# Three steps of the layer norm: from two GpSimd instructions to three ScalarE instructions, with new due times

## The chip, the core and the metric

The kernel runs on one core of a Trainium2 chip. Its five engines each have an in-order queue: TensorE (PE, with PEld for its weight loads), VectorE (DVE), ScalarE (ACT), GpSimd (POOL) and SyncE (SP), which here issues all DMAs. The metric is device time in microseconds of one execution; lower is better. The number shown is the median of several executions.

## What is computed

A decoder layer over 16 sequences of 256 positions and width 512. It has three parts, each added to its input and followed by a layer norm without gain or offset: a selective state-space scan (1024 channels, 16 states), a cross-attention over the feature axis (16 heads of 16 channels, sequences of 512), and a gated feed-forward part with quantized weights and activations. Cut to what matters:

```python
def _layernorm(x, axis=-1, eps=1e-05):
    m = jnp.mean(x, axis=axis, keepdims=True)
    v = jnp.var(x, axis=axis, keepdims=True)
    return (x - m) / jnp.sqrt(v + eps)

x = _layernorm(x + _L0_attn_ref(x, ...), axis=-1)    # state-space scan
x = _layernorm(x + _L0_xattn_ref(x, ctx_2048, ...), axis=-1)
x = _layernorm(x + _L0_ffn_ref(x, ...), axis=-1)
```

Inside the scan, per channel and state, `h[t] = exp(A*dt[t]) * h[t-1] + dt[t]*B[t]*u[t]`, and `y[t]` is the sum of `h[t]*C[t]` over the states.

## The kernel before, in words

A sequence (here: a batch) goes through four stages: `prep` (projections, a short convolution, the time steps), `scan`, `attn` (output projection, first norm, cross-attention, second norm) and `ffn` (feed-forward part, third norm). The stages of different batches overlap: while batch b is scanned, earlier batches are in attention and feed-forward.

The scan of a batch is cut into 32 units (8 channel tiles of 128 by 4 groups). A unit has 128 partitions of 32 channels by 4 states, and 4 states along the free axis. For a unit, a DMA brings `dtr` (time steps and products, broadcast from `dtd` in DRAM); POOL makes the first product `h <- bcr*dtr` (L657, recorded by the helper at L233); ACT makes the decays `dA` in PSUM (L668), two buffers; DVE runs two scans (L672); POOL makes the second product `h <- h*bcr` (L675, also L233). After four units PE sums over the states (L697), DVE gates (L705), and four of the seven `h` buffers are free again.

In attention PE makes scores (L830), DVE takes their maxima (L845), ACT makes exponentials (L889), PE forms the products with the values (L896). The casts L779, L781 and L854 split numbers into bf16 parts. The `rc` instruction L941 on POOL, once per batch, belongs to the softmax's denominators. The feed-forward weights are quantized once on the chip, in 24 pieces with two ACT instructions each (L439, L441). ACT changes its function table with an ACT_TABLE_LOAD, mostly around the softplus of `prep` (L595).

The order of each queue isn't written out by hand. The code makes tasks, each with a due time `t`, an engine, an estimated duration, the tasks that it comes after, and the buffers that it takes and frees. A planner, `run` (L167), goes through a clock of its own, and at each moment issues on every idle engine the ready task with the earliest due time, if its buffers are free and it isn't more than `AHEAD` beyond the earliest task not yet begun. A unit of due time is a scan unit, so a batch is 32 of them (`NSL`). The names in capitals at the top (L44 to L77) shift the due times: `KP`, `QP` and `VP` those of the attention's projections, `BCP` those of B and C in `prep`, `WEIGHP` that of the second product, `NORM`, `FFN` and `LNF` those of the second norm, the feed-forward part and the third norm, `WQ0` and `WQ` start and step of the weight quantization, `WS0` and `WS` those of the pass over the weights that finds their scale. What comes out of the planner is the order in each queue; on the chip every instruction then waits for what it needs.

The norm itself is `layernorm` (L451), called three times a batch, 48 times in all. DVE takes the statistics of two tiles of 128 positions (L458, L459); they lie in `lmv`, which holds mean and variance for each. `small` on POOL makes of them, on 128x2 numbers, the scale `lrs` and the offset `lnb`, in four instructions: L463 adds eps to the variance and takes the maximum with eps, L464 raises to the power -0.5, L465 changes the sign of the mean, L466 multiplies. ACT then applies scale and offset to the two tiles (L469).

Of the kernel before, what the change touches and what calls it, by code (L numbers as in the profile page):

```python
# [10 lines left out]
F32 = mybir.dt.float32  # L11
# [3 lines left out]
AF = mybir.ActivationFunctionType  # L15
ALU = mybir.AluOpType
# [4 lines left out]
P = 128  # L21
# [12 lines left out]
LN_EPS = 1e-5  # L34
# [15 lines left out]
OUT1 = 34.11  # L50
PSTEP = 2.02
TSP = 15.44
BCP = 9.29
KP = 34.45
QP = 37.76
VP = -3.68
SUMP = 0.16
WEIGHP = 1.88
FSTEP = 0.74
FUP = -0.18  # L60
BACK = 0.59

SHIFT = [(0, 0, 0, 0, 0, 0)] * 16
FDN = 14.54
LNF = 7.28
ATT = 39.73
SLAG = 7.79
GSTEP = 3.93
SCAN = -0.29
NORM = 81.05  # L70
FFN = 98.49
WQ = 3.57
WQ0 = 21.99
WS = 0.66
WS0 = 14.23
AHEAD = 12.29
HOP = 0.2  # L77
RINGS = {
    "xT": 2, "win": 2, "wr": 1, "wout": 1, "u": 4, "tmp": 2, "z": 2, "s": 3, "ts": 1, "bc": 1, "bcr": 3, "dtr": 4, "h": 7,
# [7 lines left out]
def decoder_kernel(ctx, tc, x, xT, ctx_in, mask, winT, wdtT, wbcT, wdpT, woutT, dvec, wqkvT, bqk, bv, wguT, wdnT, out):  # L87
    nc = tc.nc
# [16 lines left out]
    def const(shape, dt, s):  # L105
        return cp.tile(shape, dt, tag=s, name=s)
# [37 lines left out]
    def task(t, eng, us, fn, after=(), take=(), free=(), kb=0):  # L144
        if any(h.tag == "ps" for h in free) and eng in ("DVE", "ACT"):
            t -= BACK
        k = Task()
        k.t, k.i, k.eng, k.us, k.fn, k.take, k.free, k.kb = t, len(tasks), eng, us, fn, take, free, kb
        k.then, k.begun = [], False
        k.left = len(after)  # L150
        for p in after:
            p.then.append(k)
        for h in take:
            h.first = k
        for h in free:
            h.users += 1
        tasks.append(k)
        return k
# [5 lines left out]
    def dma(t, fn, after=(), take=(), free=(), kb=8):  # L164
        return task(t, "SP", 0.5, fn, after, take, free, kb)

    def run():  # L167
# [14 lines left out]
        while left:  # L182
# [10 lines left out]
            while f0 < len(front) and front[f0].begun:  # L193
                f0 += 1
            limit = front[f0].t + AHEAD
            any_ = False
# [56 lines left out]
    for i in range(RINGS["dA"]):  # L253

        t = ps.tile([P, 2, L], F32, tag=f"dA{i}", name=f"dA{i}", bufs=1)
# [7 lines left out]
    def cut(t, a, b):  # L263
        return t.rearrange("p (a b) -> p a b", a=a, b=b)
# [12 lines left out]
    nc.vector.memset(mhalf, -0.5)  # L277
    nmag = const([P, 1], F32, "nmag")
    nc.vector.memset(nmag, -MAGIC)
    pmag = const([P, 1], F32, "pmag")  # L280
    nc.vector.memset(pmag, MAGIC)

# [10 lines left out]
    for g in range(NB4):  # L293
# [7 lines left out]
        for n in range(1, NB4):  # L301
            t = cut(free["tmp"][n % 2][:, : NDT * NS // NB4], NDT, NS // NB4)
# [97 lines left out]
    def setup_w():  # L400
# [6 lines left out]
        for j in range(24):  # L407
            t = WS0 + WS * j
            h = Hold("hq")
# [8 lines left out]
        pb, hn = Hold("ps"), Hold("o")  # L418
        t = WS0 + WS * 24

# [13 lines left out]
        for j in range(24):  # L434
            t = WQ0 + WQ * j
            h, q = Hold("hq"), Hold("fw")
# [14 lines left out]
    def layernorm(t, hx, after):  # L451

        hst, hmv, hrs, hnb = (Hold(k) for k in ("lst", "lmv", "lrs", "lnb"))
        r = lambda: cut(hx.t, 2, H)

        def stats(i):
            st, mv = cut(hst.t, 2, 6), cut(hmv.t, 2, 2)
            nc.vector.bn_stats(st[:, i, :], r()[:, i, :])  # L458
            nc.vector.bn_aggr(mv[:, i, :], st[:, i, :])  # L459

        def small():
            mv, rs, nb = cut(hmv.t, 2, 2), hrs.t, hnb.t
            nc.gpsimd.tensor_scalar(mv[:, :, 1], mv[:, :, 1], LN_EPS, LN_EPS, ALU.add, ALU.max)  # L463
            nc.gpsimd.tensor_tensor(rs, mv[:, :, 1], mhalf, ALU.pow)  # L464
            nc.gpsimd.tensor_scalar(mv[:, :, 0], mv[:, :, 0], -1.0, None, ALU.mult)  # L465
            nc.gpsimd.tensor_tensor(nb, mv[:, :, 0], rs, ALU.mult)  # L466

        def scale(i):
            nc.scalar.activation(r()[:, i, :], r()[:, i, :], AF.Identity, bias=hnb.t[:, i : i + 1], scale=hrs.t[:, i : i + 1])  # L469

        s0 = task(t, "DVE", 0.85, lambda: stats(0), tuple(after[0]), (hst, hmv), (hst,))
        s1 = task(t, "DVE", 0.85, lambda: stats(1), (s0,) + tuple(after[1]), (), (hst,))
        m = task(t, "POOL", 1.35, small, (s0, s1), (hrs, hnb), (hmv,))
        return [task(t, "ACT", 0.79, lambda i=i: scale(i), (m,), (), (hrs, hnb)) for i in range(2)]

    S = [{} for _ in range(NB)]
# [17 lines left out]
    def prep(b):  # L494
# [72 lines left out]
        t_ts = task(t, "ACT", 0.37, lambda: nc.scalar.copy(hts.t, pts.t[:, :L]), (m,), (), (pts,))  # L567
        m = task(T + PREP + BCP, "PE", 1.1, bc, U + (t_wbc,), (p2, hbc, hp2))
        m = task(T + PREP + BCP, "ACT", 0.37, lambda: nc.scalar.copy(hp2.t, p2.t[:, :L]), (m,), (), (p2,))
        m = task(T + PREP + BCP, "PE", 0.5, lambda: nc.tensor.matmul(p3.t[:32, :L], sel4, hp2.t, start=True, stop=True), (m,), (p3,), (hp2,))  # L570
        m = task(T + PREP + BCP, "ACT", 0.36, lambda: nc.scalar.copy(hbc.t, p3.t[:32, :L]), (m,), (), (p3,))
        m = dma(t + 0.5, bc_store, (m,), (), (hbc,), 32)
# [41 lines left out]
    def scan(b):  # L614
# [29 lines left out]
        for d in range(NDT):  # L644
            hs, ws = [], []
            for g in range(NB4):
# [36 lines left out]
                for h2 in range(2):  # L683
                    ha = Hold("dA")
                    a = task(t - 0.6 + 0.5 * h2, "ACT", 0.92, lambda h2=h2, ha=ha, f=decay: f(h2, ha), (f,), (ha,), (hd,))
                    rs.append(task(t + 0.5 * h2, "DVE", 1.14, lambda h2=h2, ha=ha, f=run_: f(h2, ha), (a, p1), (), (ha,)))
                ws.append(task(t + WEIGHP, "POOL", 2.34, weigh, tuple(rs) + (st["t_C"],), (), (st["C"],)))
            pb = Hold("ps")
# [22 lines left out]
    def attn(b):  # L711
# [13 lines left out]
        for hf in range(2):  # L725
# [3 lines left out]
            for lt in range(2):  # L729
# [12 lines left out]
                m = task(t, "PE", 3.45, mult, (t_w,) + tuple(st["t_y"][4 * hf : 4 * hf + 4]), (pb,), (hw, st["u"][hf]))  # L742
                adds[lt].append(task(t, "DVE", 0.61, add, (m, t_x1), (), (pb,)))
        t_n1 = layernorm(U + OUT1 + 1.3, hr, adds)


# [40 lines left out]
        for m in range(2):  # L787
            qkproj(m, 1, T + KP + 1.05 * m)
        for m in range(2):
# [3 lines left out]
        for s in range(4):  # L793
            t = T + att + SLAG + VP + 0.7 * s
            pb = Hold("ps")
# [131 lines left out]
        no = (n0, n1)  # L927
        t = T + NORM + SHIFT[b][4]
        SO = tuple(t_so)
# [14 lines left out]
        for i in range(2):  # L944
# [9 lines left out]

            t_n.append([task(t, "POOL", 2.54, norm, (l,), (), (no[i],))])
        st["t_n2"] = layernorm(t + 1, hr, t_n)


    def ffn(b):
        st = S[b]  # L960
        T = b * NSL + FFN + SHIFT[b][5]
        hr = st["x"]
# [71 lines left out]
        for t in range(2):  # L1034
# [59 lines left out]
            m = m[0]  # L1094
            t_d.append([task(Et + 1, "DVE", 0.74, add, (m,), (), (pb, ho))])
        t_e = layernorm(E + LNF, hr, t_d)
        dma(E + LNF + 0.5, lambda: nc.sync.dma_start(out=out[b].rearrange("(k p) h -> p k h", p=P), in_=x2()), tuple(t_e), (), (hr,), 512)

# [54 lines left out]
def _build(v):  # L1153
    import numpy as np
    import concourse.bacc as bacc

    nc = bacc.Bacc("TRN2", target_bir_lowering=False, num_devices=1)
    arrays, args = {}, []
    for name, a in _layout(v):
        a = np.ascontiguousarray(a)  # L1160
        arrays[f"in_{name}"] = a
        args.append(nc.dram_tensor(f"in_{name}", a.shape, mybir.dt.from_np(a.dtype), kind="ExternalInput").ap())
    args.append(nc.dram_tensor("out_0", v["x"].shape, F32, kind="ExternalOutput").ap())
    with tile.TileContext(nc, schedule_with_timeline_sim=True) as tc:
        decoder_kernel(tc, *args)
    return nc, arrays
# [10 lines left out]
```

## Time and profile before

| | |
|---|---|
| median of 3 runs | 3010.79 us (3008.86 to 3011.28) |
| the profiled execution | 3007.98 us, span 3005.8 us |
| mean granted TensorE clock | 0.965 |
| DVE scans (L672) | 1024 x 1208 ns |
| POOL products (L233, 128x1024) | 1012 x 2363 ns |
| ACT decays (L668) | 2048 x 475 ns |
| POOL, norm: L463, L464, L465, L466 | 48 each: 231, 708, 228, 195 ns |
| ACT, norm: L469 | 96 x 806 ns |
| DVE, norm: L458, L459 | 96 each: 676, 182 ns |

The profile is of one execution. "Busy" is the time from an instruction's start to its end; instructions of one engine can overlap a little, so the distance from start to start can be shorter than the duration (a 128x1024 product on POOL takes 2363 ns and the next one starts 2.31 us after it). A wait is the idle time of an engine before an instruction, with the instruction that ended it. The chain of waits follows the last instruction back to what released it, step by step.

### The profile page before, as it was taken

What the parts mean: (1) busy time and instruction counts of PE and PEld (TensorE: products, weight loads), DVE (VectorE), ACT (ScalarE), POOL (GpSimd) and SP (SyncE); (2) the same over time, 40 slices, a digit from 0 to 9 for tenths busy, and PEclk for the clock granted to TensorE, in tenths of its full rate; (3) what the DMA queues carried; (4) which work ended last, traced back from release to release, by engine and by line L of the source; (5) the groups of instructions that cost most, each with busy time, mean ns of one, the idle gap of its engine ahead of it and who ended that gap; (6) DMA issues with size and microseconds to landing.
All of it is one profiled execution on the core that took longest, in us unless ns stands there. A gap on an engine that the chain in (4) does not pass through costs nothing.

```text
span 3005.8 us, 51881 instructions
## 1 busy us (share of the span) xinstructions
PE 2650.5 (88%) x17514; PEld 1319.4 (44%) x17514; DVE 2674.1 (89%) x4043; ACT 2334.0 (78%) x4731; POOL 2596.5 (86%) x1435
## 2 busy tenths in 40 slices
PE   6567888999989999898999989899998999999995
PEld 4333443454545445444444544444353544434333
DVE  6969888999989999898999989899999989999873
ACT  4787978787787878778787877878788787888674
POOL 3899999999898999989899998989989899999311
PEclk9787999999999999999999999999999999999998
DMA  6695776566465665746665574656646566564432
GB/s 215 222 305 182 233 224 205 188 199 206 143 218 182 204 195 171 224 138 214 193 200 186 168 224 150 216 189 196 189 157 226 165 203 193 187 203 147 125 98 71
DMA packets 363250, 567.46 MB, mean 189 GB/s; under 512 B 47316, under 2 KB 200024, under 8 KB 358888
## 3 DMA queue, kind: packets, MB, share of 16 engines
q1 hardware_dynamic: 362984, 564.16, 58.2%
q8 instruction: 137, 2.24, 0.3%
q14 instruction: 129, 1.06, 0.1%
HBM read 449.61 MB, written 114.43 MB: 188 GB/s over the span
## 4 chain that ended last, share of the span: by engine, by line
POOL 28%; PE 27%; DVE 16%; ACT 13%; issue 10%; DMA 5%; SPq 1%; POOLq 0%; ACTq 0%; DVEq 0%
POOL h L233 23%; DVE h L672 7%; PE bank L491 6%; ACT pT L889 4%; PE bank L697 4%; DVE mx L845 4%; PE av L896 3%; PE bank L830 3%; ACT dA L668 3%; PE bank L1013 3%; PE bank L763 2%; PE bank L799 2%; DMA dtr<-dtd 2%; ACT xres L469 1%; POOL s L233 1%
## 5 line engine op out<-in xcount | busy, mean ns | idle before, releaser
L672 DVE TENSOR_TENSOR_SCAN h<-dA,h 128x512 f32<-128x512 f32 x1024 | 1223.3, 1208 | 83.0 <-POOL h L233 41.2
L233 POOL TENSOR_TENSOR h<-h,bcr 128x1024 f32<-128x1024 f32 x512 | 1207.9, 2363 | 95.7 <-DVE h L672 92.9
L233 POOL TENSOR_TENSOR h<-bcr,dtr 128x1024 f32<-128x1024 f32 x500 | 1177.7, 2363 | 69.9 <-PE bank L697 63.4
L668 ACT ACTIVATE dA<-dtr,A 128x255 f32<-128x255 f32 x2048 | 963.9, 475 | 297.1 <-DVE h L672 255.6
L830 PE MATMUL bank<-qk 108*128 108x512 bf16 x2003 | 616.3, 385 | 78.9 <-DVE mx L845 44.7
L845 DVE TENSOR_REDUCE mx<-bank 128x1 f32<-128x512 f32 x1004 | 655.1, 675 | 25.8 <-PE bank L830 25.6
L889 ACT ACTIVATE pT<-bank 128x512 f32<-128x512 f32 x999 | 566.6, 590 | 119.1 <-PE bank L830 113.9
L491 PE MATMUL bank<-xT,win 128*128 128x256 f32 x1984 | 454.5, 382 | 20.4 <-DVE u L520 7.8
L896 PE MATMUL av<-pT,vaug 128*32 128x256 f32 x4096 | 336.2, 397 | 106.6 <-ACT pT L889 104.5
L491 PEld LDWEIGHTS bank<-xT,win 128*128 128x128 f32 x1984 | 377.2, 192 | 83.8 <-DVE u L520 9.5
L830 PEld LDWEIGHTS <-qk 108*128 108x128 bf16 x2048 | 179.7, 98 | 392.2 <-issue 264.2
L697 PE MATMUL bank<-h,sel 128*32 128x256 f32 x4096 | 262.0, 399 | 49.0 <-POOL h L233 48.9
L1013 PE MATMUL bank<-fw,xqT 128*128 128x512 fp8e4 x976 | 248.5, 381 | 12.5 <-DVE hq L1023 4.0
L896 PEld LDWEIGHTS av<-pT,vaug 128*32 128x32 f32 x4096 | 88.8, 109 | 356.8 <-ACT pT L889 277.9
L736 PE MATMUL bank<-wout,u 128*128 128x512 f32 x512 | 231.0, 595 | 4.9 <-DVE u L705 4.4
L697 PEld LDWEIGHTS bank<-h,sel 128*32 128x32 f32 x4096 | 124.1, 114 | 180.9 <-POOL h L233 72.2
L517 DVE SCALAR_TENSOR_TENSOR tmp<-bank,cw,tmp 128x254 f32<-128x254 f32 (+2 forms) x384 | 165.1, 468 | 7.8 <-ACT tmp L510 7.7
L1013 PEld LDWEIGHTS <-xqT 128*128 128x128 bf16 x1024 | 96.3, 98 | 151.4 <-issue 57.6
L736 PEld LDWEIGHTS bank<-wout,u 128*128 128x128 f32 x512 | 96.0, 190 | 108.5 <-issue 94.4
L1086 PE MATMUL bank<-fw,s 128*128 128x512 fp8e4 x496 | 127.0, 380 | 1.8 <-ACT s L1077 1.1
L233 POOL TENSOR_TENSOR s<-s,u 128x512 f32<-128x512 f32 x64 | 80.7, 1272 | 39.9 <-ACT s L595 39.9
L705 DVE TENSOR_TENSOR u<-bank,z 128x256 f32<-128x256 f32 x128 | 52.8, 413 | 60.9 <-PE bank L697 60.8
(157 smaller groups left out, 2961.7 us busy)
## 6 DMA issues: line engine op xcount, KB each, us to landing
dtr<-dtd SPq DMA_DIRECT2D x512, 256.0 KB
win<-in_winT SPq DMA_DIRECT2D x124, 512.0 KB
qk<-sqk SPq DMA_DIRECT2D x128, 384.0 KB
dtd<-s SPq DMA_DIRECT2D x64, 512.0 KB
wout<-in_woutT SPq DMA_DIRECT2D x32, 1024.0 KB
fw<-gu_q SPq DMA_DIRECT2D x64, 512.0 KB
sqk<-qf SPq DMA_DIRECT2D x64, 384.0 KB
bcr<-bcd SPq DMA_DIRECT2D x32, 512.0 KB
```

The source lines that it names most:

```text
L233: return nc.gpsimd.tensor_tensor(out, a, b, ALU.mult)
L491: nc.tensor.matmul(ps_t[:, i * L : (i + 1) * L], ws[:, k, i * P : (i + 1) * P], xt[:, k, :], start=k == 0, stop=k == 3)
L517: nc.vector.scalar_tensor_tensor(zi, pb.t[:, i * L : (i + 1) * L - s], cw[:, d0 + i, j : j + 1], zi, ALU.mult, ALU.add)
L668: nc.scalar.activation(ha.t[:, i, 1:], hd.t[:, 1:L], AF.Exp, scale=A[:, d, g, j : j + 1])
L672: nc.vector.tensor_tensor_scan(seg, ha.t.rearrange("p n l -> p (n l)"), seg, 0.0, ALU.mult, ALU.add)
L697: m = nc.tensor.matmul(pb.t[DB * g : DB * g + DB, :L], sel, cut(hs[g].t, J, L)[:, j, :], start=False, stop=j == J - 1, tile_position=(0, D ...
L736: nc.tensor.matmul(pb.t, u[:, i, lt * P : (lt + 1) * P], wo()[:, i, :], start=i == 0, stop=i == 3)
L830: nc.tensor.matmul(pb.t, qk()[:, j, side, c * P : (c + 1) * P], qk()[:, j, 1 - side, :], start=True, stop=True)
L845: task(t, "DVE", 0.62, lambda pb=pb, c=c, j=j: nc.vector.tensor_reduce(mx()[:, j, c : c + 1], pb.t, AX.X, ALU.max), (m,), (), (pb,))
L889: V["x"] = nc.scalar.activation(hp.t[:, j * H : (j + 1) * H], pb.t, AF.Exp, scale=DSC)
L896: i = nc.tensor.matmul(hav.t[32 * k : 32 * k + 32, :], vaug_f[:, c, c0 : c0 + 32], hp.t[:, j * H + h * L : j * H + (h + 1) * L], start=c == 0,
L1013: nc.tensor.matmul(pb.t, xqT()[:, i, t * P : (t + 1) * P], wu()[:, k, i, :], start=i == 0, stop=i == 3)
```

## The change

In `layernorm` the two POOL instructions L463 and L465 go. In their place a new task `signs` on ACT, with an estimated duration of 0.65, does three activations on the same 128x2 numbers: the sign of the mean, a Relu of the variance, and the addition of eps, whose bias is a new constant `leps`. It comes after the statistics, and `small`, now two instructions with an estimate of 0.9, comes after it. Eleven numbers that set due times change with it, and `AHEAD`.

```diff
-BCP = 9.29
-KP = 34.45
+BCP = 9.42
+KP = 34.95
-VP = -3.68
+VP = -3.24
-WEIGHP = 1.88
+WEIGHP = 2.11
-LNF = 7.28
+LNF = 7.66
-NORM = 81.05
-FFN = 98.49
-WQ = 3.57
-WQ0 = 21.99
-WS = 0.66
-WS0 = 14.23
-AHEAD = 12.29
+NORM = 82.79
+FFN = 99.13
+WQ = 2.31
+WQ0 = 23.46
+WS = 0.64
+WS0 = 16.0
+AHEAD = 15.36
...
+    leps = const([P, 1], F32, "leps")
+    nc.vector.memset(leps, LN_EPS)
...
+        def signs():
+
+            mv = cut(hmv.t, 2, 2)
+            nc.scalar.activation(mv[:, :, 0], mv[:, :, 0], AF.Identity, scale=-1.0)
+            nc.scalar.activation(mv[:, :, 1], mv[:, :, 1], AF.Relu)
+            nc.scalar.activation(mv[:, :, 1], mv[:, :, 1], AF.Identity, bias=leps)
+
         def small():
             mv, rs, nb = cut(hmv.t, 2, 2), hrs.t, hnb.t
-            nc.gpsimd.tensor_scalar(mv[:, :, 1], mv[:, :, 1], LN_EPS, LN_EPS, ALU.add, ALU.max)
             nc.gpsimd.tensor_tensor(rs, mv[:, :, 1], mhalf, ALU.pow)
-            nc.gpsimd.tensor_scalar(mv[:, :, 0], mv[:, :, 0], -1.0, None, ALU.mult)
             nc.gpsimd.tensor_tensor(nb, mv[:, :, 0], rs, ALU.mult)
...
-        m = task(t, "POOL", 1.35, small, (s0, s1), (hrs, hnb), (hmv,))
+        m = task(t, "ACT", 0.65, signs, (s0, s1), (), (hmv,))
+        m = task(t, "POOL", 0.9, small, (m,), (hrs, hnb), (hmv,))
```

## The prediction

> **What bounds the kernel now.** I read the page's engine totals first, then equal stretches of the span, then the waits of the steady part, then GpSimd's timeline around one norm, then the groups of small instructions.
>
> ```profile
> PE 2650.5 (88%) x17514; PEld 1319.4 (44%) x17514; DVE 2674.1 (89%) x4043; ACT 2334.0 (78%) x4731; POOL 2596.5 (86%) x1435
> POOL 3899999999898999989899998989989899999311
> ```
>
> Three engines are within 3% of each other and none is full. POOL's tenths stand at 8 or 9 and fall off only at both ends.
>
> ```profile
> core 0: us, PE busy (x) PEld busy (x) DVE busy (x) ACT busy (x) POOL busy (x), PEclk, DMA share, GB/s
> 375.00:550.00 175.00, 152.71 (x1028) 72.05 (x1028) 152.92 (x219) 145.02 (x294) 168.35 (x90) 0.95 0.65 207
> 1425.00:1600.00 175.00, 161.30 (x1084) 81.23 (x1083) 162.91 (x246) 139.59 (x288) 162.39 (x89) 0.99 0.59 192
> 2825.00:3006.00 181.00, 144.51 (x888) 63.67 (x880) 109.32 (x204) 107.08 (x191) 19.64 (x40) 0.92 0.32 102
> ```
>
> Early (second row) POOL leads at 168 of 175 us. In the steady part PE, DVE and POOL are equal at 161 to 163. In the last 181 us POOL has almost nothing to do, so what it is relieved of there is worth nothing.
>
> ```profile
> POOL h L233 <- DVE h L672: 71.4, 30, 4.8
> POOL h L233 <- PE bank L697: 43.4, 18, 3.5
> DVE h L672 <- POOL h L233: 21.2, 31, 1.0
> DVE h L672 <- ACT dA L668: 11.0, 30, 0.7
> ACT dA L668 <- DVE h L672: 168.5, 207, 2.7
> ```
>
> These are the waits between 900 and 2650 us (total, times, longest). POOL idles 114.8 us there, 11.6 us in each period of 177.1 us (the rc instruction L941 starts at 1680.52, 1857.69, 2034.92 us). It waits for DVE's scans and for PE, which holds the h buffers. DVE waits for POOL as well: the engines take turns at being late.
>
> ```profile
> 1341.77 0.23 POOL L463 TENSOR_SCALAR lmv<-lmv 128x2 f32<-128x2 f32 x1
> 1342.08 0.71 POOL L464 TENSOR_TENSOR lrs<-lmv,mhalf 128x2 f32<-128x2 f32 x1
> 1342.85 0.23 POOL L465 TENSOR_SCALAR lmv<-lmv 128x2 f32<-128x2 f32 x1
> 1343.16 0.20 POOL L466 TENSOR_TENSOR lnb<-lmv,lrs 128x2 f32<-128x2 f32 x1
> 1343.31 2.36 POOL L233 TENSOR_TENSOR h<-h,bcr 128x1024 f32<-128x1024 f32 x1
> ```
>
> One norm holds POOL from 1341.77 to 1343.31, 1.54 us, with no wait inside.
>
> **What is removed.** L463 and L465 cost 0.31 us each from start to next start. That is 0.62 us a norm, three norms a period: 1.86 us of 177.1, and 48 x 0.62 = 29.8 us in all. Adding start-to-start durations along POOL's built order gives 2578.4 us up to the last h product before and 2552.4 after: 26.0 us can count, the rest lies in the tail, where POOL idles.
>
> **What is added.** Three activations on 128x2 a norm. No such row exists.
>
> ```profile
> L414 ACT ACTIVATION_READ_ACCUMULATOR hq<-hq 128x1 f32 x24 | 4.5, 186 | 0.0
> L854 ACT ACTIVATE ml<-bank 8x128 bf16<-8x128 f32 x242 | 61.6, 254 | 3.4 <-DVE bank L859 1.3 <-PE bank L874 0.9
> L595 ACT ACT_TABLE_LOAD x31 | 39.8, 1283 | 0.6
> L439 ACT ACTIVATE hq<-hq,pmag,wiv 128x1024 f32<-128x1024 f32 x24 | 29.5, 1234 | 7.2 <-DMA hq<-in_wdnT 3.7 <-DMA hq<-in_wguT 3.5
> ```
>
> The nearest in width is the 128x1 read at 186 ns, the next the 8x128 activation at 254 ns: 0.56 to 0.76 us a norm if each ends before the next starts. I take 0.56, since width sets more than rows; it is 27 us of ACT in all (upper end 36). ACT has 139.6 of 175 us busy, so its total covers this. If that cover fails, 1.7 us a period falls on ACT's followers.
>
> The Trainium skill's page "ScalarE: Activation LUTs" (Rules for kernel authors) speaks against the edit: relu, add and multiply belong on VectorE. By its section on what a table load costs (186 ns fixed, 93 ns more for a pointer operand, 93 ns overlap), my estimate is 0.47 to 0.66 us for the three; no run here shows that. The trace stands against it here: in the steady row above DVE is busy 162.9 of 175 us and ACT 139.6, so VectorE has 23 us less room.
>
> **The new wait.** The three stand in ACT's in-order queue and wait for the second statistics (L459). Behind them in the built order come decays (L668), exponentials (L889) and casts (L854, L779); DVE's scans wait for the first, PE's value products for the second. The hop itself is short: L459 ends at 2998.88 and L463 starts at 2998.97, 0.09 us. A norm's latency becomes 1.54 - 0.62 + 0.56 + 0.09 = 1.57 us, so the tail's norms and the last one change by nothing.
>
> **What moves.** The due times are changed too, so every queue has another order. The counts below come from the two built orders with the trace's start-to-start durations (h product 2.31 us, scan 1.13, score maximum 0.60).
>
> Head: ACT's work ahead of the first decay goes from 23.8 to 27.2 us, as there are two table loads more (65 against 63) and one tanh earlier; and SP's queue has the 0.77 MB of wqkv ahead of the first dtr, which was behind it. POOL's first product waits for that dtr now (4.87 us). I take +3.5; ends 0 (all hidden) and +8 (wqkv at the 171 GB/s of the first 45 us is 4.6 more).
>
> Batch 1: of the 48 quantizing activations (L439, L441, about 1.1 us each) 44 fall into it, against 23. ACT's queue there grows from 133.4 to 158.0 us and passes POOL's 153.9. Now batches 1 and 2 take 158.6 and 169.2 us, 4.1 and 7.7 more than their fullest queue (POOL 154.5 and 161.5). Batch 1 thus becomes 162 to 166: +3.5 to +7, I take +5. Batch 2 has POOL at 160.2: -1.
>
> Batches 3 to 14: POOL's queue falls from 164.3 to 162.4 a batch, DVE's stays 163.6, PE's 160.3. But the work comes in larger lumps. Before, the most DVE work from one scan unit to the next is 10.3 us; after, it is 13.3 (batches 4 to 7) and 13.9 (9 to 14), and GpSimd's order changes from one repeated pattern to two. To weigh this I cut a batch into stretches of eight scan units, take in each the longest of the ACT, DVE and POOL queues, and average over where the cuts lie. Before this gives 175.6 us a batch, against 177.1 measured, so it follows the trace within 1%. Summed over batches 3 to 14 the change is -0.7 us; with POOL level with the scans instead of one unit behind, +3.5; with stretches of four units, -4.1 and +23.7. I take +4; ends -4 and +24. The 1.86 us a period are thus given back: in a shorter POOL queue the wait for DVE and PE grows.
>
> Last batch and tail: after the last scan DVE has 122.8 us left before and 122.2 after, PE 160.9 and 160.3: 0.
>
> Sum: +3.5 + 5 - 1 + 4 + 0 = +11.5 us. On the profiled execution's 3007.98 us (span 3005.8 and 2.2 around it) this is 3019.5; that execution lies 2.8 us below the median of 3010.79, on which the sum gives 3022.3. I take 3020 us.
>
> **Rivals.** *The relief is kept.* If the lumps are absorbed by the seven h buffers, only DVE and POOL matter. The largest lead of a POOL product over its scan and back within a batch is 8.5 us before, and 8.0 (batches 4 to 7) and 9.5 (9 to 14) after. Batch by batch, POOL's queue plus this gives 16.7 us less over batches 1 to 14, or 26 if no wait grows: 2994, at best 2985. For it: POOL is 168 of 175 early, and ACT has room. Against it: in the steady part POOL already waits for two engines whose work stays.
>
> *Swallowed exactly.* Steady -4, head and batch 1 half hidden (+4): 3011. For it: the tables above cancel almost to zero. Against it: the ACT queue of batch 1 has no cover.
>
> *ACT's lumps reach the scans.* There are two dA buffers, so decay and scan cannot drift more than two scans apart. If the stretches of four units are right, +24, with 3.5 + 5 - 1 of head and first batches: 3010.8 + 31.5 = 3042. It decides if DVE waits for dA more than 3 us a period (now 11.0 us in ten). Against it: the wait is small now with lumps of 10 us.
>
> The edit itself not being made is excluded: the built order has 48 times three activations, and 96 GpSimd instructions fewer.
>
> **How the numbers follow.** 0.2% is 6 us, about what a measurement of this kernel can tell from no change. Forecast (given back, and the start paid: 3012 to 3032) 0.37; lumps reach the scans 0.17; swallowed 0.14; kept 0.32. A time over 3016.8 takes nearly all of the first two: slower 0.52. Faster, under 3004.8: 0.33. Within: 0.15. The forecast's own range is 3012 to 3032. Cases of both signs hold most of the chance, so the range reaches from 2986 (nearly all of the relief) to 3045 (all lumps, the head near its upper end).
>
> **What would show it.** Right: POOL idles over 13 us in a steady period and the period is 176 to 178 us; batch 1 takes over 162 us with ACT leading; the first h product starts after 52 us. Wrong: a steady period under 175.5 us means that the relief is kept; activations of the norm over 0.3 us each, or waits of the scans for dA over 3 us a period, mean the third rival; an unchanged start falsifies the head.

## The result, and the profile after

| | before | after |
|---|---|---|
| median | 3011.03 us (3008.86 to 3011.81, 4 runs) | 3040.3 us (3034.92 to 3042.04, 4 runs) |
| ratio | | 1.0096, 95% interval 1.0082 to 1.011 |
| span of the profiled execution | 3005.8 us | 3040.2 us |
| mean granted TensorE clock | 0.965 | 0.960 |

The changed kernel is 29 us slower, 1%. The lines below stand against those of the kernel before; the eight new lines of code make L668 into L676, L672 into L680, L697 into L705, and the norm is now L460 to L476. First the page: the engine totals, GpSimd's tenths (the busy share of each fortieth of the span), and the chain of waits by engine (before, that chain was POOL 28%, PE 27%, DVE 16%, ACT 13%, DMA 5%).

```profile
PE 2682.7 (88%) x17514; PEld 1323.3 (44%) x17514; DVE 2676.0 (88%) x4044; ACT 2356.5 (78%) x4877; POOL 2574.1 (85%) x1339
...
POOL 3899999999898999989898997989899798989211
...
DVE 31%; PE 23%; POOL 19%; DMA 10%; issue 9%; ACT 7%; SPq 1%; POOLq 0%; ACTq 0%; DVEq 0%
```

POOL has 96 instructions and 22.4 us of busy time less (48 times the 231 and 228 ns of the two steps), ACT 146 instructions and 22.5 us more (144 activations and two table loads): the move itself is there. Yet the span is 34 us longer, and GpSimd's steady part shows sevens where there were eights and nines. Next the equal stretches:

```profile
core 0: us, PE busy (x) PEld busy (x) DVE busy (x) ACT busy (x) POOL busy (x), PEclk, DMA share, GB/s
...
200.00:375.00 175.00, 143.21 (x861) 67.14 (x861) 148.17 (x203) 157.51 (x291) 168.50 (x78) 0.87 0.76 247
375.00:550.00 175.00, 156.21 (x1056) 74.06 (x1058) 158.93 (x232) 138.53 (x300) 173.22 (x89) 0.96 0.63 195
1425.00:1600.00 175.00, 158.17 (x1075) 79.20 (x1074) 162.34 (x244) 137.73 (x293) 159.79 (x83) 0.99 0.60 190
2825.00:3006.00 181.00, 157.36 (x998) 64.18 (x990) 119.89 (x219) 116.01 (x228) 27.72 (x39) 0.95 0.33 104
```

The same stretch of 200 to 375 us before, which the prediction does not show:

```profile
200.00:375.00 175.00, 147.75 (x876) 70.75 (x875) 154.92 (x218) 144.23 (x279) 166.65 (x81) 0.89 0.69 226
```

From 200 to 375 us ACT is busier, as predicted (157.5 us; before 144.2), but POOL is at 168.5 and leads. In the steady part (1425 to 1600 us) PE does 3.1 us less in 175 us than before, POOL 2.6 (of which 1.4 are the steps moved away, three norms of 0.46) and DVE 0.6: nobody has become the bound, and the engines wait more. The last row still holds work that was done by then before. The waits from 900 to 2650 us (total, times, longest) say for whom:

```profile
ACT dA L676 <- DVE h L680: 133.7, 160, 3.5
...
POOL h L233 <- DVE h L680: 88.7, 44, 4.7
...
POOL h L233 <- PE bank L705: 55.7, 34, 2.9
...
ACT hq L1024 <- PE bank L1021: 46.7, 44, 2.6
DVE mx L853 <- PE bank L838: 38.9, 36, 2.7
...
PE bank L705 <- POOL h L233: 34.1, 28, 2.9
...
DVE h L680 <- POOL h L233: 13.8, 18, 1.4
```

Three of the same waits before, which the prediction does not show:

```profile
PE bank L697 <- POOL h L233: 11.5, 10, 1.6
ACT hq L1016 <- PE bank L1013: 11.4, 20, 0.7
...
DVE mx L845 <- PE bank L830: 8.1, 29, 0.4
```

POOL waits 17 us more for the scans and 12 more for PE's sums. But PE's sums also wait for POOL (34.1; before 11.5), DVE's maxima for PE's scores (38.9; before 8.1), and ACT's `hq`, made of a result of the feed-forward part, for PE (46.7; before 11.4). Each of these engines is late for another one.

Where the 34.4 us of span went, read from the start of every 32nd second product on POOL (one batch each; the differences are taken before rounding):

| stage | before | after | difference | predicted |
|---|---|---|---|---|
| start to the first second product | 57.2 | 64.3 | +7.1 | +3.5 (0 to 8) |
| batch 0 | 140.0 | 137.8 | -2.1 | not counted |
| batch 1 | 158.6 | 160.3 | +1.7 | +5 (3.5 to 7) |
| batch 2 | 169.2 | 160.8 | -8.4 | -1 |
| batches 3 to 14 | 2119.9 | 2147.8 | +28.0 | +4 (-4 to 24) |
| batch 15, to the last second product | 155.3 | 162.0 | +6.7 | 0 |
| tail | 205.8 | 207.2 | +1.4 | 0 |

### The profile page after: what moved, and what is told of

Same layout as the page of the kernel before. It is cut to its first block, busy times and chain, and to the rows that moved or that the text cites. A ratio compares the mean times of both kernels' runs of the same rounds, so it can differ in the third digit from the quotient of the medians.

```text
span 3040.2 us, 51841 instructions
## 1 busy us (share of the span) xinstructions
PE 2682.7 (88%) x17514; PEld 1323.3 (44%) x17514; DVE 2676.0 (88%) x4044; ACT 2356.5 (78%) x4877; POOL 2574.1 (85%) x1339
## 4 chain that ended last, share of the span: by engine, by line
DVE 31%; PE 23%; POOL 19%; DMA 10%; issue 9%; ACT 7%; SPq 1%; POOLq 0%; ACTq 0%; DVEq 0%
POOL h L233 16%; DVE h L680 13%; DVE mx L853 8%; PE bank L705 5%; PE bank L499 4%; PE bank L838 3%; PE av L904 2%; ACT dA L676 2%; ACT pT L897 2%; DVE tmp L525 2%; PE bank L1021 2%; DMA qk<-sqk 2%; DVE hq L1033 1%; DVE hq L1031 1%; PE bank L744 1%
## 5 line engine op out<-in xcount | busy, mean ns | idle before, releaser
L680 DVE TENSOR_TENSOR_SCAN h<-dA,h 128x512 f32<-128x512 f32 x1024 | 1220.0, 1207 | 58.0 <-POOL h L233 28.7
L676 ACT ACTIVATE dA<-dtr,A 128x255 f32<-128x255 f32 x2048 | 966.5, 475 | 254.7 <-DVE h L680 206.4
L853 DVE TENSOR_REDUCE mx<-bank 128x1 f32<-128x512 f32 x999 | 648.5, 675 | 58.4 <-PE bank L838 57.5
L838 PE MATMUL bank<-qk 108*128 108x512 bf16 x1996 | 626.3, 388 | 79.3 <-DVE mx L853 35.2
L499 PE MATMUL bank<-xT,win 128*128 128x256 f32 x1984 | 464.3, 388 | 19.5 <-ACT hq L416 14.3
L499 PEld LDWEIGHTS bank<-xT,win 128*128 128x128 f32 x1984 | 382.5, 195 | 92.1 <-ACT hq L416 14.6
L904 PE MATMUL av<-pT,vaug 128*32 128x256 f32 x4096 | 334.3, 399 | 67.1 <-ACT pT L897 64.3
L705 PE MATMUL bank<-h,sel 128*32 128x256 f32 x4096 | 273.5, 412 | 61.1 <-POOL h L233 60.5
L705 PEld LDWEIGHTS bank<-h,sel 128*32 128x32 f32 x4096 | 127.3, 117 | 200.2 <-POOL h L233 91.3
L1024 ACT ACTIVATE hq<-bank,fhc 128x512 f32<-128x512 f32 x122 | 83.1, 684 | 65.8 <-PE bank L1021 64.9
L702 PE MATMUL bank<-u,diag 32*32 32x256 f32 x1024 | 85.4, 405 | 51.8 <-DVE z L646 24.3
```

Of the source, the lines that this page charges most:

```text
L499: nc.tensor.matmul(ps_t[:, i * L : (i + 1) * L], ws[:, k, i * P : (i + 1) * P], xt[:, k, :], start=k == 0, stop=k == 3)
L676: nc.scalar.activation(ha.t[:, i, 1:], hd.t[:, 1:L], AF.Exp, scale=A[:, d, g, j : j + 1])
L680: nc.vector.tensor_tensor_scan(seg, ha.t.rearrange("p n l -> p (n l)"), seg, 0.0, ALU.mult, ALU.add)
L705: m = nc.tensor.matmul(pb.t[DB * g : DB * g + DB, :L], sel, cut(hs[g].t, J, L)[:, j, :], start=False, stop=j == J - 1, tile_position=(0, D ...
L838: nc.tensor.matmul(pb.t, qk()[:, j, side, c * P : (c + 1) * P], qk()[:, j, 1 - side, :], start=True, stop=True)
L853: task(t, "DVE", 0.62, lambda pb=pb, c=c, j=j: nc.vector.tensor_reduce(mx()[:, j, c : c + 1], pb.t, AX.X, ALU.max), (m,), (), (pb,))
```

## The norm itself, after

ACT's timeline around one norm in the steady part, then POOL's:

```profile
1527.97 0.20 ACT L466 ACTIVATE lmv<-lmv 128x2 f32<-128x2 f32 x1 [0.51 <-DVE lmv L461]
1528.08 0.19 ACT L467 ACTIVATE lmv<-lmv 128x2 f32<-128x2 f32 x1
1528.30 0.29 ACT L468 ACTIVATE lmv<-lmv,leps 128x2 f32<-128x2 f32 x1
1528.50 0.55 ACT L518 ACTIVATE tmp<-bank,cw 128x256 f32<-128x256 f32 x1
```

```profile
1529.26 0.70 POOL L472 TENSOR_TENSOR lrs<-lmv,mhalf 128x2 f32<-128x2 f32 x1
1530.04 0.20 POOL L473 TENSOR_TENSOR lnb<-lmv,lrs 128x2 f32<-128x2 f32 x1
1530.19 2.39 POOL L233 TENSOR_TENSOR h<-h,bcr 128x1024 f32<-128x1024 f32 x1
```

The three activations last 0.20, 0.19 and 0.29 us, 0.68 in all, but the second starts before the first has ended and the next instruction before the third has: from the first start to the next instruction's start it is 0.53 us (predicted 0.56). POOL is held from 1529.26 to 1530.19, 0.93 us instead of 1.54, so 0.61 is saved (predicted 0.62). ACT waited 0.51 us for the statistics here; over the whole run that wait is 15.0 us in 20 times. In the last norm of all, the time from the end of the last statistics to ACT's `xres` is 1.75 us (3033.26 to 3035.01) against 1.72 before.

The estimate from the Trainium skill's page "ScalarE: Activation LUTs" (What ACT_TABLE_LOAD costs) was 0.47 to 0.66 us for the three. Its parts are near the rows: 186 ns fixed against 190 and 197 measured, and 93 more for an operand against the 296 ns of L468, which has the bias `leps`. The overlap of 93 ns shows between the first step and the second, but not between the second and the third, which starts 0.03 us after the second has ended.

So the move costs and saves what the rows of before said. The question is the 29 us.

## Experiments

The change does two things at once: it moves two steps, and it changes twelve planner numbers and the tasks, so that every queue gets another order. Theory 1: the order makes it slower, and the move alone is a gain. Theory 2: the three activations and their wait for the statistics hold up ScalarE's in-order queue, and so the rest.

**The order alone, first by its numbers.** The kernel before, with the twelve new numbers (`BCP` to `AHEAD`) and nothing else of the change.

```diff
-BCP = 9.29
+BCP = 9.42
...
-AHEAD = 12.29
+AHEAD = 15.36
```

> The twelve new numbers (eleven due times and AHEAD) with the norm as before, four steps on GpSimd. Theory 1 (the order that the due times make costs the time): 3030 to 3050 us, near the changed kernel's 3040. Theory 2 (the three activations and the new wait on ScalarE cost it): 3005 to 3016 us, like before.

3077.39 us, 1.0218 of before (1.0198 to 1.0238). The direction is theory 1's, the size more than expected: with four POOL steps the new numbers cost 66 us, more than the whole change. It is an order of its own, though: without a task on ACT for the norm, the planner doesn't arrive at the changed kernel's.

**The move with the old numbers.** The changed code (its own ACT task `signs`) with the twelve old numbers. The planner sees an ACT task more and makes a third order of it, again one repeated pattern.

```diff
-NORM = 82.79
+NORM = 81.05
...
-AHEAD = 15.36
+AHEAD = 12.29
```

> The three steps on ScalarE as their own task, with all twelve numbers as before; the planner makes an order of its own from them. Theory 1: 2995 to 3025 us, on either side of before, since a third order comes out and only its lumps decide. Theory 2: 3030 us or more.

3031.76 us, 1.0065 (1.0048 to 1.0081). Old numbers don't bring the old order back, and this order too is slower than before's. It lies 7 us above theory 1's range and within theory 2's, so this run alone does not part the two. The new numbers can't be all of the loss: both plans made with the ACT task lie above before.

**The move at exactly the old order.** The three activations are emitted inside the POOL task `small`, so the planner plans what it did before; the two GpSimd steps are gone. Apart from these steps every queue has before's order, instruction by instruction.

```diff
-            nc.gpsimd.tensor_scalar(mv[:, :, 1], mv[:, :, 1], LN_EPS, LN_EPS, ALU.add, ALU.max)
+            nc.scalar.activation(mv[:, :, 0], mv[:, :, 0], AF.Identity, scale=-1.0)
+            nc.scalar.activation(mv[:, :, 1], mv[:, :, 1], AF.Relu)
+            nc.scalar.activation(mv[:, :, 1], mv[:, :, 1], AF.Identity, bias=leps)
             nc.gpsimd.tensor_tensor(rs, mv[:, :, 1], mhalf, ALU.pow)
-            nc.gpsimd.tensor_scalar(mv[:, :, 0], mv[:, :, 0], -1.0, None, ALU.mult)
```

> Every queue in exactly the order of before; the two GpSimd steps of the norm are gone and the three activations stand in ScalarE's queue at that place. Theory 1: the move by itself is harmless and worth part of the 26 us of GpSimd: 2985 to 3011 us. Theory 2: 3025 us or more, with the scans waiting for dA more than now.

2994.31 us, 0.9939 (0.9918 to 0.9961): faster than both kernels, 16.6 us under the 3010.93 of before in the same session, and 46 under the changed kernel, which does the same instructions in another order. Its waits from 900 to 2650 us:

```profile
POOL h L233 <- DVE h L675: 80.2, 34, 4.8
POOL h L233 <- PE bank L700: 43.5, 16, 3.5
...
DVE mx L848 <- PE bank L833: 11.7, 23, 1.8
ACT hq L1019 <- PE bank L1016: 11.4, 20, 0.7
...
DVE h L675 <- ACT dA L671: 10.0, 23, 0.7
...
PE bank L700 <- POOL h L233: 6.9, 6, 1.4
```

POOL's wait for the scans has grown by 9 us in 1750 against before (it is done earlier), and the rest is as before. The longer waits that the changed kernel shows among PE, DVE, POOL and ACT are absent.

**Exactly the new order, without the move.** The changed kernel with `signs` empty and the four steps back on POOL; all else in its order.

```diff
         def signs():
-            mv = cut(hmv.t, 2, 2)
-            nc.scalar.activation(mv[:, :, 0], mv[:, :, 0], AF.Identity, scale=-1.0)
...
+            pass
...
+            nc.gpsimd.tensor_scalar(mv[:, :, 1], mv[:, :, 1], LN_EPS, LN_EPS, ALU.add, ALU.max)
             nc.gpsimd.tensor_tensor(rs, mv[:, :, 1], mhalf, ALU.pow)
+            nc.gpsimd.tensor_scalar(mv[:, :, 0], mv[:, :, 0], -1.0, None, ALU.mult)
```

> Every queue in exactly the order of the changed kernel, but with the norm's four steps on GpSimd and none on ScalarE. Theory 1: the order stays, and GpSimd is 26 us fuller: 3040 to 3065 us. Theory 2: 3011 to 3025 us, since ScalarE is free of the three steps.

3075.76 us, 1.0209 (1.0191 to 1.0227), 11 us above theory 1's range and far from theory 2's. With this the square is closed:

| | old order | new order | order costs |
|---|---|---|---|
| four steps on POOL | 3011 (before) | 3076 | +65 |
| two on POOL, three on ACT | 2994 | 3040 (after) | +46 |
| the move brings | -17 | -35 | |

The move is a gain in both orders, the order a loss with both sets of steps. In the new order the move brings 35 us, about twice as much as in the old one; that this is more than the 29.8 us of POOL that it takes away lies within the noise of the two ratios (some 7 us). One line of the waits of this kernel shows what it shortens there:

```profile
ACT xres L473 <- POOL lnb L470: 41.0, 28, 2.3
```

In the changed kernel the same wait is 10.0 us, and 20.0 in the run below without the three activations: in the new order ACT stands at the scaled tiles until POOL's four steps are through, and with two of them less it stands there half as long. How much of the 35 us this makes was not tried.

**ScalarE's steps alone, in both orders.** The two kernels with the move, each without its three activations: the sign of the mean and eps are left out of the computation.

```diff
-            nc.scalar.activation(mv[:, :, 0], mv[:, :, 0], AF.Identity, scale=-1.0)
-            nc.scalar.activation(mv[:, :, 1], mv[:, :, 1], AF.Relu)
-            nc.scalar.activation(mv[:, :, 1], mv[:, :, 1], AF.Identity, bias=leps)
```

> The order of before in every queue, the two GpSimd steps gone and the three activations of the norm gone too: sign and eps are left out of the computation. Theory order (the three activations cost next to nothing, the order costs all): 48 x 0.68 = 33 us of ScalarE go, on an engine that is busy 78% of the span, so the time stays within 6 us of the run with the three activations at this order (2994.3): 2988 to 2997. Theory wait (what stands behind the three activations on ScalarE is held up by their wait for the statistics): it falls by 10 us or more, under 2984.

> The changed kernel's order in every queue, with the three activations of the norm left out (sign and eps are not computed). Theory order: within 10 us of the changed kernel (3040.3): 3030 to 3042, and about as far above the run of the old order without activations as the changed kernel lies above the old order with them (46 us). Theory wait (in this order the three activations stand ahead of decays that the scans need, so the wait for the statistics is the loss): 20 us or more below the changed kernel, under 3020, and the gap between the orders shrinks to 25 us or less.

Old order: 2985.18 us, 0.9917 (0.9902 to 0.9932), 9 us under the kernel with the activations. That lies between the two expectations, and the intervals of the two ratios overlap, so it is a cost of some 9 us and not a sharp one. New order: 3038.95 us, 1.0098 (1.0081 to 1.0115), 1.4 us under the changed kernel, which is nothing that can be told. The gap between the orders is 54 us without the activations, not smaller than with them. Theory 2 falls for the changed kernel: no ScalarE step of the norm and no wait for the statistics makes its loss.

**What in the new order costs it.** Three suspicions, each tried as a pair: the same relief in the old order (with the move) and in the changed kernel. If the relieved resource is what the new order runs short of, the changed kernel gains far more than the other. Called B, C and D: TensorE, VectorE, and the stores of `qf` (projected queries and keys) to DRAM and back, which the chain of waits of the changed kernel passes in the steady part. In the expectations A stands for GpSimd and the scans as the pace of both orders, E for a loss among the compute engines alone.

```profile
2168.92 5.01 DMA sqk<-qf
2173.93 0.01 issue
2173.94 5.98 DMA qk<-sqk
2179.92 0.14 issue
2180.06 0.81 PE bank L838 x3
```

B leaves out a quarter of the input projections (three of four k slices; 512 matmuls L499 less):

```diff
-            for k in range(4):
+            for k in range(3):
```

> Order of before with the three activations (the 2994 us kernel), and every projection by 3 of its 4 slices of the inner dimension (a quarter of it is left out): TensorE has 512 passes of 0.22 us less, 113 us, 7 us a batch. Theory A (in either order GpSimd and the scans pace it): 2985 to 2996 us. Theory B (TensorE being late is what the new order pays): a little less here too, 2975 to 2990.

> The changed kernel with the same quarter of the projections left out. Theory A: 3025 to 3040 us, a gain like that of the old order, under 15 us. Theory B: 2970 to 3005 us, a gain of over 35 us and more than twice that of the old order, since the scores behind the state sums in TensorE's queue come earlier.

2979.85 us in the old order (0.99, 0.9884 to 0.9917), 14 less than with all four; 3049.27 in the new one (1.0139, 1.0118 to 1.016), 9 more. The old order's time lies within what B had for it, the new order's outside both ranges; a gain in the new order above that of the old, B's sign, is absent. The relief was smaller than meant, though: 76 us of busy time in the old order (2643.7 to 2568.0) and 62 in the new one (2682.7 to 2620.8), against 113. The stretch from 900 to 2650 us of the changed kernel, and of the changed kernel with the relief:

```profile
900.00:2650.00 1750.00, 1602.74 (x10645) 797.91 (x10646) 1610.89 (x2413) 1381.95 (x2903) 1582.70 (x820) 0.99 0.59 186
```

```profile
900.00:2650.00 1750.00, 1553.96 (x10273) 741.28 (x10272) 1597.94 (x2399) 1365.41 (x2879) 1569.23 (x814) 0.96 0.58 185
```

With less to do, TensorE was granted 0.96 instead of 0.99, and the other engines got through less as well. So this is weak evidence against B: the relief was partly given back.

C takes the score maxima over 384 of 512 columns:

```diff
-nc.vector.tensor_reduce(mx()[:, j, c : c + 1], pb.t, AX.X, ALU.max)
+nc.vector.tensor_reduce(mx()[:, j, c : c + 1], pb.t[:, :384], AX.X, ALU.max)
```

> Order of before with the three activations, and the score maxima over 384 of 512 columns (the rest is left out): VectorE has about 1024 x 0.13 = 136 us less, 8.5 us a batch. Theory C (VectorE's lumps pace the steady part): 2950 to 2975 us. Theory A with GpSimd alone: 2985 to 2994.

> The changed kernel with the maxima over 384 columns. Theory C (the larger lumps of VectorE are what the new order pays): 2960 to 2995 us, a gain of 45 us or more and well above that of the old order. Theory B (TensorE): 3010 to 3035, no more than in the old order.

2973.97 us (0.9884, 0.9869 to 0.9899) and 3016.06 (1.0023, 1.0011 to 1.0034, 10 runs): 20 us and 24 us less for 113 and 117 us of VectorE work less (busy 2673.4 to 2560.4 and 2676.0 to 2559.0). In the old order that is what C had expected, in the new one it is far from C's 45 us or more. The gap stays at 42. VectorE's work matters alike in both orders; it isn't what tells them apart.

D leaves the stores out from batch 2 on; the loads read what the first batches stored:

```diff
+                if b < 2:
+                    nc.sync.dma_start(out=dst, in_=src)
-                nc.sync.dma_start(out=dst, in_=src)
```

> Order of before with the three activations, without the stores of projected queries and keys (sqk<-qf) from the third batch on, 168 transfers fewer; the loads qk<-sqk stay and read old values. Theory D (in the new order transfers stand on the chain that sets the period; in the profiles their share of the chain is 7% here and 10% there): 2982 to 2996 us, a gain of at most 12 us. Theory E (the new order loses among the compute engines alone): the same 2982 to 2996.

> The changed kernel without the same stores. Theory D: 2995 to 3015 us, a gain of 25 us or more, since the 5 us store and 6 us load that its chain runs through in each period fall to one load. Theory E: 3028 to 3040 us, a gain like that of the old order.

2987.5 us (0.9929, 0.9912 to 0.9946) and 3044.26 (1.0107, 1.0086 to 1.0128): 7 less in the old order and 4 more in the new one, neither clear. The transfers stand in the chain, but taking them away brings the new order nothing: D falls. That a piece stands in the chain does not make it the cause.

TensorE's clock is a rival that no run settles. Its mean was 0.968 for the move in the old order and 0.960 in the changed kernel, and TensorE's busy time 2643.7 and 2682.7 us for the same matmuls. Even if all of these 39 us counted, they would not make up the 46. At the rate of B in the old order, 14 us for 76 us of busy time, they are worth 7 by my estimate.

What the runs do show of the loss is a set of waits that goes with the order, whatever the steps (us in total, 900 to 2650 us):

| wait | before | move, old order | after | after without activations | new order, four steps on POOL |
|---|---|---|---|---|---|
| POOL's products for the scans | 71.4 | 80.2 | 88.7 | 87.2 | 91.5 |
| POOL's products for PE's sums | 43.4 | 43.5 | 55.7 | 54.1 | 53.0 |
| PE's sums for POOL's products | 11.5 | 6.9 | 34.1 | 33.8 | 39.3 |
| DVE's maxima for PE's scores | 8.1 | 11.7 | 38.9 | 39.5 | 37.0 |
| ACT's `hq` for PE | 11.4 | 11.4 | 46.7 | 46.6 | 48.6 |
| DVE's scans for ACT's decays | 11.0 | 10.0 | 5.6 | 6.6 | 10.4 |

The loss lies mostly where these waits are: batches 3 to 14 take 2111.8 us with the move in the old order and 2147.8 in the changed kernel, 36 us more. The first two columns' kernels and the last three's differ in how POOL's queue is cut. Counted in the timeline from 900 to 2650 us, with POOL's other instructions left aside, the first and second products of the kernel before come in 513 stretches of one kind (mean 1.23 products, 30 of them with three or four), those of the changed kernel in 425 (mean 1.47, 62 with three or four). The move with the old numbers, 37 us above the same move at the old order, has 1.46 too. A reading that fits, but was only argued: with products in bunches, PE's sums, each of which needs four units, come late (third row); what is behind them in PE's queue is late for DVE and ACT (fourth and fifth rows), and POOL waits longer for both. The third order, of the move with the old numbers, weakens this reading: its products are bunched as much (70 stretches with three or four), but PE's sums wait only 15.3 us for POOL there and `hq` 2.1 us for PE, and batches 3 to 14 take 2134.8 us. So the same waits don't make its loss, and bunches alone don't rank the orders. Which placement costs how much was not tried one by one and stays open. Shown is that the loss lies in the order, not in a step of the norm nor in the stores, and that relief of VectorE doesn't close the gap.

## Why the prediction was right or wrong

The forecast was 3020 us within 2986 to 3045, slower the likeliest side; 3040.3 came out. The side and the stated range hold; the forecast's own range, 3012 to 3032, does not, and its mechanism (given back, and the start paid) holds only in part. The first product comes late, as said, and POOL idles longer. But the start as a whole is not paid: from the beginning to the first second product of batch 3 the changed kernel is 1.7 us ahead, where +7.5 had been summed. And the relief isn't given back by longer waits of a shorter POOL queue: at a fixed order the move gains 17 us (old) or 35 us (new). What takes more than that away is the order, with 46 to 65 us, and batches 3 to 14 end 28 us longer. That 3040 lies inside 2986 to 3045 is in part luck, since the upper end was set by a rival whose mechanism the waits exclude.

- *What is removed and added*: right. 0.61 us of POOL a norm (0.62 predicted), 0.53 us of ACT (0.56), and a last norm that takes 0.03 us longer. The 26.0 us that were said to be able to count do count where the order is kept and ScalarE's steps are left out: 27 us (3012.42 to 2985.18).
- *The new wait*: said to cost little. Right in the changed kernel (1.4 us with all three steps), some 9 us in the old order, which the sum had no term for.
- *Head, +3.5 (0 to 8)*: +7.1, the cause for the most part as described and the size at the upper end. In the changed kernel a tanh with its two table loads stands between the two halves of the softplus, so the second `dtd` store leaves SP at 51.69 us instead of 46.55, and the first four `dtr` loads are issued from 53.02 on instead of 46.97 (0.9 us of this is a wait of SP for a `win` load). From the first of these issues to POOL's first product it is 5.40 us instead of 3.77. That product waits for `dtr`:

```profile
58.42 4.66 POOL L233 TENSOR_TENSOR h<-bcr,dtr 128x1024 f32<-128x1024 f32 x2 [4.48 <-DMA dtr<-dtd]
```

- *Batch 1, +5 with ACT leading; batch 2, -1*: +1.7 and -8.4. The step "ACT's queue there grows from 133.4 to 158.0 us and passes POOL's 153.9" was right of the queue (157.5 us busy in 175) and wrong of its effect: the batch took 160.3 us, and POOL at 168.5 of 175 led on. Batch 2, from which the shift takes quantizing activations, gained eight times what I had credited; why so much was not tried.
- *Batches 3 to 14, +4 (-4 to 24)*: +28.0, the mis-sized term, just beyond its upper end. The longest queue in stretches of eight scan units gave -0.7 or +3.5, by where POOL was placed against the scans, and in stretches of four -4.1 or +23.7. A spread that wide was the sign that the method can't rank two orders, and I took a figure near its coarse end. That the eight-unit figure met before's level (175.6 against 177.1) was taken as proof of it, but a level that fits says nothing of a difference between two orders. A stretch assumes that engines meet only at its ends; the trace shows them meeting inside, in the waits of the table above. A finer stretch was no cure by itself, as the -4.1 shows. POOL idles about 16 us in a period of 179 (159.7 us in 1750, counted as the prediction's 114.8; predicted over 13 in 176 to 178), so POOL's longer idling was foreseen, its cause was not.
- *Last batch and tail, 0*: +6.7 and +1.4. Equal totals of work were read as equal time; the order of the last batch costs as the others do.
- *The relief is kept (2994)*: wrong for the changed kernel, and to the microsecond what the move does at the old order. The microsecond is luck: that sum used the leads of the new order. The price of the move was well worked out; what I did not work out separately was the price of the order, 46 us, against which it stands.
- *ACT's lumps reach the scans (3042)*: its time nearly came, its mechanism did not. The sign for it was a wait of the scans for `dA` over 3 us a period; it fell from 11.0 to 5.6 us in ten periods, and leaving the activations out changes nothing that can be told:

```profile
DVE h L680 <- ACT dA L676: 5.6, 15, 0.7
```

- *Swallowed exactly (3011)*: excluded by the interval.

## What to carry to other kernels

Where an order is planned from due times, a small edit is two changes: the instructions and the order. Price them apart, by emitting the new instructions in the old order first: here the move is worth 0.6%, and the re-planned order takes 1.5% away. With three in-order engines each 85 to 90% busy, totals per batch did not rank the orders here. The waits between pairs of engines told the old order from the new one, with several pairs waiting longer at once; they did not explain the third order.

## What had not been expected of the hardware

The same instructions in two orders differ by 46 us (1.5%) to 65 us (2.1%), with busy totals of every engine within 2%. TensorE with 512 matmuls less had a lower granted clock, and more so in the new order: 0.968 fell to 0.957 in the old one, 0.960 to 0.941 in the new one; there the sums L705 took 440 ns instead of 412, and a quarter of the input projections less made the kernel 9 us slower. And the three activations of the norm, 0.68 us in all, held ScalarE for 0.53 us: the second starts 0.11 us after the first, which works on the other half of the tile, and the third, which reads what the second wrote, 0.22 us after it.
